# Splitting the last list of expert slots: broken slots first, full ones after the copy to the output

## The chip, the cores and the metric

The kernel runs on one core of a Trainium2 chip. Times are device microseconds of one execution. A core has five engines with a queue each: TensorE (PE in the profile, its weight loads PEld), VectorE (DVE), ScalarE (ACT), GpSimd (POOL) and SyncE (SP). SP issues most plain DMAs, POOL issues the indirect ones: a gather of rows by a list of indices, and a store that adds to the rows it names.

## What is computed

One decoder layer on 16 sequences of 128 tokens of 256 numbers, in float32: attention over latents, a recurrent mixing with a context, and a mixture of 8 experts, each behind a layer norm, each added to its input. Only the last matters here. Every token goes to its two best experts:

```python
logits = x @ router_w.T
routing_weights, selected = sparsemixer_eval(logits, JITTER_EPS)   # two of 8 experts a token
for e in range(E):
    h = jax.nn.silu(x @ w_gate[e].T) * (x @ w_up[e].T)
    out = out + dense_w[:, e:e + 1] * (h @ w_down[e].T)
return x + out
```

That gives 4096 entries (token, expert) for the 2048 tokens. How many an expert gets is known only at run time.

## The kernel before

**Steps.** The program is one loop over steps s, written out in full. Steps 0 to 63 are the attention's units (four a sequence); mixing, layer norm and routing of a sequence follow some steps behind its attention. From step 64 (SLOT0) on, each step also does one *slot* of the experts: up to 128 entries of one expert. In each step there are four places, "pre", "A", "B" and "C", in which a plan (`at(step, place, function)`) hangs further work. Every engine works off its instructions in the order of this loop; no scheduler moves them.

**Lists.** Routing (`route`) writes each entry (token, weight) to its expert's list in DRAM, with indirect DMAs of POOL. The sum before the experts lies in the DRAM tensor `acc`, its normed rows in `xn2`. Which expert and which part of its list a slot takes is worked out at run time on VectorE by `table`, in some twenty small instructions that are spread over several places. `list_slots` then reads the start of a slot's entries into registers and loads the 128 entries (SP, L849).

**Tables.** Because at least so many full slots are sure once 8 and 12 sequences are routed, the first 17 slots (SF) are taken early, from tables "0" and "1". When all are routed there are two more tables. Table "3" has 8 slots (S3) that are certainly full. Table "2" has 14 (S2): all that is left, each expert's remaining full slots and then its broken one, and as many of the 14 as there are entries for. Table "3" runs last. Of table "2", 11 slots always run (an unused one works on blank entries) and the last 3 (`RARE`, SKIP = 3) stand under a run-time condition, `if_used`, which compares the number of used slots with k on all five engines. A skipped slot's body is replaced by instructions that raise the semaphores as the body would have. So 17 + 11 + 8 = 36 slots always run, in the order of `ORDER`, and the three guarded ones are placed between the 28th and the 29th of them.

**One slot.** In step j of the slots: `fetch` gathers the rows of the slot three places ahead (POOL, L898, into xr); `bring` copies the next slot's expert weights (ACT and DVE, L920); `up` makes the products pg and pu (PE, L966), SiLU (ACT, L976) and hT (DVE, L978); then come the works of place "C"; `turn` transposes the next slot's rows (PE, L928) and copies them to xT (DVE, L930); `down` makes the last product pd of the slot before (PE, L988), scales it to y (DVE, L999) and adds it to its rows (POOL, L1004). Place "B" stands ahead of fetch, bring and up. `turn` of the slot after and `down` of the slot before thus lie between two `up`s on TensorE.

**The copy.** The adding stores of all slots but the last 8 go to `acc`. At the first of the last 8, SP copies `acc` to the output (L1001, 2 MB from DRAM to DRAM), and these 8 add to the output itself. Every add waits for the one before it, since both may name the same row. `y` has three buffers, `xr` four.

The diff touches the tables (`last_table`, `very_last`), the guard (`if_used`), `down` and the plan.

Of the kernel before, what the change touches and what calls it, by code (L numbers as in the profile page):

```python
# [9 lines left out]
F32 = mybir.dt.float32  # L10
# [8 lines left out]
P = 128  # L19
B = 16  # L20
T = 128
N = B * T
C = 256
# [3 lines left out]
E = 8  # L27
# [25 lines left out]

def sure(b):
    return (2 * b * T - E * (P - 1) + P - 1) // P

# [1 line left out]
FIRST_B = (8, 12)  # L60
S1 = [sure(FIRST_B[0]), sure(FIRST_B[1]) - sure(FIRST_B[0])]
SF = sum(S1)
S3 = 8
assert SF + S3 <= sure(B)
S2 = (2 * N + E * (P - 1)) // P - SF - S3
NS = SF + S2 + S3


SKIP = 3
RARE = range(SF + S2 - SKIP, SF + S2)  # L70
ORDER = [j for j in range(NS) if j not in RARE]

SLOT0 = NU
# [6 lines left out]
def decoder_kernel(  # L80
# [19 lines left out]
    nc = tc.nc  # L100

    const = ctx.enter_context(tc.tile_pool(name="const", bufs=1))
# [25 lines left out]
    def bank(tag, name, bufs=2):  # L128
        return psum.tile([P, 512], F32, tag=tag, name=name, bufs=bufs)
# [68 lines left out]
    ebase = const.tile([P, E], F32, tag="ebase", name="ebase")  # L198
    before = const.tile([P, P], F32, tag="before", name="before")
    ones = const.tile([P, P], F32, tag="ones", name="ones")  # L200
    iotas = const.tile([P, max(*S1, S2, S3)], F32, tag="iotas", name="iotas")
    seg = const.tile([P, E], F32, tag="seg", name="seg")

    taken = const.tile([P, E], F32, tag="taken", name="taken")
# [30 lines left out]
    def constants():  # L235
        for t, step, base in ((rev, -1, E), (eid, 1, 0), (ebase, N, 0)):
            nc.gpsimd.iota(
                t,
                pattern=[[step, E]],
                base=base,  # L240
                channel_multiplier=0,
                allow_small_or_imprecise_dtypes=True,
            )

        nc.gpsimd.memset(before, 1.0)
        nc.gpsimd.affine_select(
            out=before,
            in_=before,
            compare_op=ALU.is_gt,
            fill=0.0,  # L250
            base=0,
            pattern=[[1, P]],
            channel_multiplier=-1,
        )
        nc.gpsimd.memset(ones, 1.0)
        nc.gpsimd.iota(
            iotas,
            pattern=[[1, max(*S1, S2, S3)]],
            base=0,
            channel_multiplier=0,  # L260
            allow_small_or_imprecise_dtypes=True,
        )
        nc.gpsimd.memset(seg, 1.0)
        nc.gpsimd.memset(taken, 0.0)

        nc.gpsimd.memset(blank, 0)
        place = blank[:, :, 1]
        nc.gpsimd.iota(place, pattern=[[1, QL]], base=0, channel_multiplier=QL)
        nc.vector.tensor_single_scalar(place, place, P - 1, ALU.bitwise_and)
        nc.vector.tensor_single_scalar(place, place, N, ALU.bitwise_or)  # L270
# [478 lines left out]
    def whole(c, add, name):  # L749

        f = rp.tile([P, E], F32, tag=f"wf{name}", name=f"wf{name}")
        nc.vector.tensor_scalar_add(f, c, float(add))
        i = rp.tile([P, E], I32, tag=f"wi{name}", name=f"wi{name}")
        nc.vector.tensor_copy(i, f)
        nc.vector.tensor_single_scalar(i, i, 7, ALU.logical_shift_right)
        nc.vector.tensor_copy(f, i)
        return f
# [111 lines left out]
    def last_table():  # L869

        cnt = counts("2")
        full = whole(cnt, 0, "3")
        nc.vector.tensor_sub(full, full, took[0])
        yield
        last = share(full, S3, "3")
        both = rp.tile([P, E], F32, tag="both", name="both")
        nc.vector.tensor_add(both, took[0], last)
        took.append(last)
        yield
        left = whole(cnt, P - 1, "2")  # L880
        nc.vector.tensor_sub(left, left, both)
        yield from table(S2, left, both, "2")

    making = {}

# [21 lines left out]
    hpools, xTs, hTs, regs, useds, brought = [], {}, {}, {}, [], {}  # L907
# [22 lines left out]
        nc.vector.tensor_copy(xT, pt[:, : NC * P].rearrange("p (c t) -> p c t", c=NC))  # L930
        xTs[j] = xT

    def if_used(j, work):

        t, k = slots[j]
        if not useds:
            _, v = nc.values_load_multi_w_load_instructions(
                t["used"],
                engines=[
                    mybir.EngineType.PE,  # L940
                    mybir.EngineType.Activation,
                    mybir.EngineType.DVE,
                    mybir.EngineType.Pool,
                    mybir.EngineType.SP,
                ],
                min_val=0,
                max_val=S2,
                skip_runtime_bounds_check_because="no more than all",
            )
            useds.append(v[0])  # L950
        with tc.If(useds[0] > k):
            work(j)

    def up(j):
        t, k = slots[j]
# [25 lines left out]
    def down(j):  # L981
        e = regs.pop(j)
        hT = hTs.pop(j)
        pd = bank("mm", f"pd_{j}")

        def products():
            for f in range(NF):
                nc.tensor.matmul(  # L988
                    pd[:, :C],
                    hT[:, f, :],  # L990
                    wall[:, bass.ds(e, 1), WD0 + f * C : WD0 + (f + 1) * C],
                    start=(f == 0),
                    stop=(f == NF - 1),
                )

        products()
        en = entries.pop(j)
        y = hpools[0].tile([P, C], F32, tag="y", name=f"y_{j}", bufs=3)
        nc.vector.tensor_scalar_mul(y, pd[:, :C], en[:, 2:3].bitcast(F32))  # L999
        if j == SF + S2:  # L1000
            nc.sync.dma_start(out2, acc[0:N, :])  # L1001

        def add():
            nc.gpsimd.indirect_dma_start(  # L1004
                out=acc if j < SF + S2 else out2,
                out_offset=bass.IndirectOffsetOnAxis(ap=en[:, 1:2], axis=0),
                in_=y,
                in_offset=None,
                compute_op=ALU.add,
            )  # L1010

        add()


    plan = {}
# [1 line left out]
    def at(step, place, fn, *args):  # L1017
        plan.setdefault((step, place), []).append((fn, args))
# [106 lines left out]
    for b in range(B):  # L1125
        s = NHG * b
        if b + 1 < B:
            at(s + 2, "pre", load_ctx, b + 1)
        at(s + 1, "C", wkv_exps, b)
        at(s + 2, "B", wkv_back, b)  # L1130
        at(s + 3, "A", wkv_back_add, b)
        at(s + 4, "B", wkv_forth, b)
        at(s + 5, "A", wkv_forth_add, b)
        at(s + 5, "B", project, b, (0, 1))
        at(s + 6, "B", project, b, (2, 3))
        at(s + 6, "C", rest_values, b)
        at(s + 7, "B", project, b, (4, 5))
        at(s + 7, "C" if b < B - 1 else "B", project, b, (6, 7, NP))
        for name, (step, place) in {B - 2: last_but_one, B - 1: last}.get(b, usual).items():
            at(s + step, place, stages[name], b)  # L1140
        if b < E:
            for k in range(3):
                at(s + 11 + k, "C", load_expert, b, k)
        if b % RB == RB - 1:
            r = b // RB
            parts = ((13, "B"), (13, "C"), (14, "B"), (15, "B"), (15, "C"))
            if b == B - 1:
                parts = ((12, "B"), (12, "C"), (13, "B"), (14, "B"), (14, "C"))
            for step, place in parts:
                at(s + step, place, route_part, r)  # L1150
            for k in range(2 * RB):
                if b < B - 1:
                    at(s + 16 + k, "A", route_part, r)
                else:
                    at(s + 15 + k // 4, "AC"[k // 2 % 2], route_part, r)
        if b + 1 in FIRST_B:
            i = FIRST_B.index(b + 1)
            for k in range(6):
                at(s + 18 + k, "C", table_part, i, first_table, i)
            for k in range(0, S1[i], 2):  # L1160
                at(s + 24 + k // 2, "C", list_slots, min(2, S1[i] - k))
        if b == B - 1:
            for k in range(7):
                at(s + 15 + k // 3, "ABC"[k % 3], table_part, "2", last_table)
            for k in range(0, S2, 4):
                at(s + 17 + k // 4, "C", list_slots, min(4, S2 - k))
            for k in range(4):
                at(s + 20 + k, "B", table_part, "3", very_last)
            for k in range(0, S3, 4):
                at(s + 24 + k // 4, "C", list_slots, min(4, S3 - k))  # L1170
    for j in range(AHEAD):
        at(SLOT0 - 2 + (j + 1) // 2, "A", fetch, j)

# [31 lines left out]
    def whole_slot(j):  # L1205
        fetch(j)
        bring(j)
        turn(j)
        up(j)
        down(j)  # L1210

    for s in range(SLOT0 + len(ORDER) + 1):
        j = s - SLOT0
# [44 lines left out]
        if j >= 0:  # L1258
            ahead(j + 1, turn)
            if j >= 1:  # L1260
                down(ORDER[j - 1])
        if j == SF + S2 - SKIP:
            for r in RARE:
                if_used(r, whole_slot)
    assert not plan and len(slots) == NS


# [52 lines left out]
```

## Time and profile before

| | us |
|---|---|
| median of three runs | 571.44 |
| lowest, highest | 567.83, 572.62 |
| the profiled execution's own time | 571.29 |
| its span in the profile | 569.6 |

```profile
PE 523.7 (92%) x3317; PEld 447.1 (78%) x3334; DVE 326.8 (57%) x831; ACT 293.7 (52%) x891; POOL 326.6 (57%) x379
## 2 busy tenths in 40 slices
PE   4989999999999999999998959989999999998990
...
POOL 5355656574787665688636873544486545451532
PEclk9999999999999999999997979999999999999996
```

The first line is the busy time of each engine, its share of the span and its instructions. The digits below are busy tenths of 40 equal slices of 14.2 us. TensorE's dip in the middle (slices 23 to 26) is where attention ends and the slots begin. The last slices are the slots alone.

The group of the products shows how many slots ran: 576 matmuls of one kind, 16 for each slot, so 36, and none of the guarded three.

```profile
L966 PE MATMUL pg<-xT,w 128*128 128x128 f32 x576 | 72.5, 280 | 11.7 <-DVE xT L930 9.8
L1004 POOL DMA_INDIRECT acc<-y,en x28 | 47.7, 1705 | 60.9 <-DVE y L999 27.5
```

### The profile page before, as it was taken

How to read it: one execution, taken by the hardware profiler on the slowest of the kernel's cores; microseconds unless marked ns; L12 is line 12 of the kernel's file. 1: busy time of each engine (PE TensorE's matmuls, PEld its weight loads, DVE VectorE, ACT ScalarE, POOL GpSimd, SP SyncE). 2: the span in 40 equal slices, each digit the busy share in tenths (PEclk: the TensorE clock that was granted, in tenths of full speed). 3: DMA queues.
4: the chain of work that ended last, by engine and by line, in shares of the span. 5: the costliest groups of instructions: out<-in, count | busy, mean ns of one | idle time of the engine just before them, and what ended most of it. 6: DMA issues, size and time to landing. Idle time of an engine off the chain costs nothing. (4 is left out here: it accounts for less than half of the span.)

```text
span 569.6 us, 10246 instructions
## 1 busy us (share of the span) xinstructions
PE 523.7 (92%) x3317; PEld 447.1 (78%) x3334; DVE 326.8 (57%) x831; ACT 293.7 (52%) x891; POOL 326.6 (57%) x379
## 2 busy tenths in 40 slices
PE   4989999999999999999998959989999999998990
PEld 3767788877877877878876648879989999998990
DVE  3435576577886678878668745555563543433330
ACT  1667776786676777767774744332322323222300
POOL 5355656574787665688636873544486545451532
PEclk9999999999999999999997979999999999999996
DMA  4422145364455544121221111233223333235321
GB/s 144 116 66 74 56 139 181 100 184 126 131 146 152 153 137 150 58 76 40 66 66 44 36 48 30 53 56 57 39 30 50 58 57 47 48 51 171 51 36 18
DMA packets 39662, 47.59 MB, mean 84 GB/s; under 512 B 14136, under 2 KB 31416, under 8 KB 39576
## 3 DMA queue, kind: packets, MB, share of 16 engines
q1 hardware_dynamic: 30106, 37.20, 22.3%
q0 software_dynamic: 7936, 9.51, 10.7%
q8 instruction: 28, 0.46, 0.4%
q10 hardware_dynamic: 1566, 0.21, 0.2%
q14 instruction: 26, 0.21, 0.1%
HBM read 28.22 MB, written 13.31 MB: 73 GB/s over the span
## 5 line engine op out<-in xcount | busy, mean ns | idle before, releaser
L466 POOL TENSOR_TENSOR pr<-pr,rsum 128x512 f32<-128x512 f32 x64 | 76.6, 1197 | 37.2 <-DVE rsum L465 27.8
L453 ACT ACTIVATE pr<-ps,nm 128x128 f32<-128x128 f32 x256 | 90.9, 372 | 10.2 <-DVE nm L445 10.1
L976 ACT ACTIVATE sl<-pg 128x512 f32<-128x512 f32 x36 | 21.5, 598 | 132.4 <-PE pg L966 128.4
L966 PE MATMUL pg<-xT,w 128*128 128x128 f32 x576 | 72.5, 280 | 11.7 <-DVE xT L930 9.8
L966 PEld LDWEIGHTS pg<-xT,w 128*128 128x128 f32 x576 | 70.7, 196 | 15.4 <-issue 14.1
L1004 POOL DMA_INDIRECT acc<-y,en x28 | 47.7, 1705 | 60.9 <-DVE y L999 27.5
L433 PEld LDWEIGHTS ps<-kvT,q 72*128 72x128 f32 x512 | 67.5, 191 | 16.2 <-issue 8.0
L506 PE MATMUL po<-outw_sb,yP 128*128 128x256 f32 x288 | 74.6, 387 | 0.0
L978 DVE TENSOR_TENSOR hT<-sl,pu 128x512 f32<-128x512 f32 x36 | 24.8, 688 | 86.1 <-PE pu L966 80.0
L433 PE MATMUL ps<-kvT,q 72*128 72x128 f32 x512 | 68.8, 276 | 4.3 <-DMA q<-qr 3.1
L966 PE MATMUL pu<-xT,w 128*128 128x128 f32 x576 | 70.5, 276 | 0.0
L988 PE MATMUL pd<-wall,hT 128*128 x288 | 68.0, 379 | 0.0
L966 PEld LDWEIGHTS pu<-xT,w 128*128 128x128 f32 x576 | 67.6, 193 | 0.0
L480 PE MATMUL py<-aT,kvN 128*72 128x512 f32 x128 | 66.6, 602 | 0.3 <-ACT aT L474 0.3
L445 DVE TENSOR_REDUCE nm<-ps 128x4 f32<-128x512 f32 x64 | 43.7, 683 | 37.7 <-PE ps L433 37.7
L398 PE MATMUL pq<-xnT,wq_sb 128*128 128x256 f32 x256 | 64.9, 385 | 0.0
L506 PEld LDWEIGHTS po<-outw_sb,yP 128*128 128x128 f32 x288 | 54.6, 194 | 12.2 <-issue 5.3
L474 ACT COPY aT<-pt 128x512 f32<-128x512 f32 x64 | 37.3, 583 | 44.4 <-PE pt L472 44.1
L988 PEld LDWEIGHTS pd<-wall,hT 128*128 128x128 f32 x288 | 52.0, 190 | 5.6
L453 ACT ACTIVATION_READ_ACCUMULATOR pr<-ps,nm 128x1 f32 x256 | 53.8, 210 | 0.0
L398 PEld LDWEIGHTS pq<-xnT,wq_sb 128*128 128x128 f32 x256 | 45.9, 194 | 4.9 <-issue 0.2
L898 POOL DMA_INDIRECT xr<-xn,en x36 | 37.2, 1034 | 13.4 <-issue 7.4
(171 smaller groups left out, 861.3 us busy)
## 6 DMA issues: line engine op xcount, KB each, us to landing
wall<-in_wg_dram SPq DMA_DIRECT2D x8, 512.0 KB
wall<-in_wu_dram SPq DMA_DIRECT2D x8, 512.0 KB
wall<-in_wd_dram SPq DMA_DIRECT2D x8, 512.0 KB
q<-q SPq DMA_DIRECT2D x16, 224.0 KB
yP<-yB SPq DMA_DIRECT2D x32, 112.0 KB
cx<-in_cx_dram SPq DMA_DIRECT2D x16, 128.0 KB
acc<-x SPq DMA_DIRECT2D x16, 128.0 KB
xn<-row SPq DMA_DIRECT2D x16, 128.0 KB
```

The source lines that it names most:

```text
L398: nc.tensor.matmul(pq[:, :GT], w[:, c, :], xnT[g][:, c, :], start=(c == 0), stop=(c == NC - 1))
L433: nc.tensor.matmul(ps[:, j, :], q[g, hg][0:L, j, ts(i, T)], kvT[g][:, ts(i, T)], start=False, stop=(j == HG - 1),)
L445: nc.vector.tensor_reduce(nm, ps, AX.X, ALU.max, negate=True)
L453: nc.scalar.activation(pr[:, j, :], ps[:, j, :], AF.Exp, bias=nm[:, j : j + 1], accum_out=sums[:, j : j + 1],)
L466: nc.gpsimd.tensor_mul(pr, pr, rsum.unsqueeze(2).to_broadcast([P, HG, T]))
L474: nc.scalar.copy(aT, pt)
L480: nc.tensor.matmul(py[:L], kvN[g][:, ts(i, L)], aTs.pop((b, hg)), start=True, stop=True)
L506: nc.tensor.matmul(pos[b][:, :C], yP[b][:, i, :], outw_sb[:, i, :], start=(i == 0), stop=(i == NP))
L898: nc.gpsimd.indirect_dma_start(out=xr, out_offset=None, in_=xn2[0 : t["rows"], :], in_offset=bass.IndirectOffsetOnAxis(ap=entries[j][:, 0: ...
L966: nc.tensor.matmul(o[:, ts(f, P)], w[:, c * F + f * P : c * F + (f + 1) * P], xT[:, c, :], start=(c == 0), stop=(c == NC - 1),)
L988: nc.tensor.matmul(pd[:, :C], hT[:, f, :], wall[:, bass.ds(e, 1), WD0 + f * C : WD0 + (f + 1) * C], start=(f == 0), stop=(f == NF - 1),)
L1004: nc.gpsimd.indirect_dma_start(out=acc if j < SF + S2 else out2, out_offset=bass.IndirectOffsetOnAxis(ap=en[:, 1:2], axis=0), in_=y, in_of ...
```

## The change

Table "2" is split in two. The new table "2" has 8 slots, one for each expert's rest (broken or empty). A new table "4" has 7 (S4 = 32 - 25): the full slots that table "3" leaves. Order and target of the adds become: 17 early slots and 8 rests to `acc`, then the copy, then up to 7 open full slots and the 8 last ones to the output. Of the open ones (`OPEN`) the first three always run, but their adding store stands under the run-time condition; the last four (`RARE`) stand under it whole. There are 40 slots (NS) instead of 39, and again 36 that always run.

The condition (now `used`, which returns the comparison) is first loaded at the first open slot's add. Counted from step 64, table "4" is made in place "C" of slot steps 14 to 18 (19 is empty), table "3" moves from place "B" of slot steps 16 to 19 to place "C" of 20 to 23, and the loads of its entries go from slot steps 20 and 21 to 24 and 25.

```diff
-S3 = 8
-S2 = (2 * N + E * (P - 1)) // P - SF - S3
-NS = SF + S2 + S3
-SKIP = 3
-RARE = range(SF + S2 - SKIP, SF + S2)
+S2 = E
+S3 = sure(B) - SF
+S4 = 2 * N // P - SF - S3
+NS = SF + S2 + S4 + S3
+SKIP = S4 - 3
+OPEN = range(SF + S2, SF + S2 + S4)
+RARE = OPEN[S4 - SKIP :]
...
         cnt = counts("2")
         full = whole(cnt, 0, "3")
+        yield
+        left = whole(cnt, P - 1, "2")
+        nc.vector.tensor_sub(left, left, full)
+        fulls.append(full)
+        yield from table(S2, left, full, "2")
+
+    def open_table():
+
+        full = fulls.pop()
         nc.vector.tensor_sub(full, full, took[0])
-        yield
         last = share(full, S3, "3")
         both = rp.tile([P, E], F32, tag="both", name="both")
         nc.vector.tensor_add(both, took[0], last)
         took.append(last)
         yield
-        left = whole(cnt, P - 1, "2")
-        nc.vector.tensor_sub(left, left, both)
-        yield from table(S2, left, both, "2")
+        nc.vector.tensor_sub(full, full, last)
+        yield from table(S4, full, both, "4")
...
-        add()
+        if j in OPEN and j not in RARE:
+
+            with tc.If(used(j)):
+                add()
+        else:
+            add()
...
-            for k in range(4):
-                at(s + 20 + k, "B", table_part, "3", very_last)
-            for k in range(0, S3, 4):
-                at(s + 24 + k // 4, "C", list_slots, min(4, S3 - k))
+            for k in range(6):
+                at(s + 18 + k, "C", table_part, "4", open_table)
+            for k in range(4):
+                at(s + 24 + k, "C", table_part, "3", very_last)
+            for n, step in ((S4, s + 24), (S3, s + 28)):
+                for k in range(0, n, 4):
+                    at(step + k // 4, "C", list_slots, min(4, n - k))
...
-        if j == SF + S2 - SKIP:
+        if j == RARE[0]:
             for r in RARE:
-                if_used(r, whole_slot)
+                with tc.If(used(r)):
+                    whole_slot(r)
```

More of the change, by code (lines that the diff above doesn't have):

```diff
@@ L62 @@
 SF = sum(S1)
-S3 = 8
-assert SF + S3 <= sure(B)
-S2 = (2 * N + E * (P - 1)) // P - SF - S3
-NS = SF + S2 + S3
-SKIP = 3
-RARE = range(SF + S2 - SKIP, SF + S2)
+S2 = E
[5 more added lines that the diff above has]
+RARE = OPEN[S4 - SKIP :]
 ORDER = [j for j in range(NS) if j not in RARE]
@@ L200, in decoder_kernel @@
     ones = const.tile([P, P], F32, tag="ones", name="ones")
-    iotas = const.tile([P, max(*S1, S2, S3)], F32, tag="iotas", name="iotas")
+    iotas = const.tile([P, max(*S1, S2, S3, S4)], F32, tag="iotas", name="iotas")
     seg = const.tile([P, E], F32, tag="seg", name="seg")
@@ L257, in constants @@
             iotas,
-            pattern=[[1, max(*S1, S2, S3)]],
+            pattern=[[1, max(*S1, S2, S3, S4)]],
             base=0,
@@ L879, in last_table @@
         yield
-        left = whole(cnt, P - 1, "2")
-        nc.vector.tensor_sub(left, left, both)
-        yield from table(S2, left, both, "2")
+        nc.vector.tensor_sub(full, full, last)
+        yield from table(S4, full, both, "4")
+    fulls = []
     making = {}
@@ L931, in turn, with used @@
         xTs[j] = xT
-    def if_used(j, work):
+    def used(j):
         t, k = slots[j]
@@ L946, in if_used @@
                 min_val=0,
-                max_val=S2,
+                max_val=S4,
                 skip_runtime_bounds_check_because="no more than all",
@@ L950, in if_used @@
             useds.append(v[0])
-        with tc.If(useds[0] > k):
-            work(j)
+        return useds[0] > k
     def up(j):
```

## The prediction

> **What bounds the kernel now.** I read the slice table first: from slice 30 on TensorE is at 9 tenths or more with the clock granted in full, so the phase after about 430 us is bound by TensorE. Below, "place n" is the n-th of the 36 slots that always run (0 to 35, in the order of ORDER), and "row(n)", "y(n)", "add(n)" are its gather of rows, its scaled result and its adding store. The chain of waits (start, length, what) ends so:
>
> ```profile
> 550.09 1.79 PE pu L966 x16
> 551.88 3.47 PE pd L988 x16
> 555.35 0.02 issue
> 555.37 0.50 DVE y L999
> 555.87 0.27 issue
> 556.14 3.72 DMA out_dram<-y,en
> ```
>
> It follows TensorE back, place by place, in steps of 5.52 us, to an idle time at 514.96. But it passes over the second limit. The timeline of POOL, with the copy from the timeline of SP:
>
> ```profile
> 497.29 1.78 POOL L1004 DMA_INDIRECT acc<-y,en  x1 [2.43 <-DVE y L999]
> ...
> 513.85 1.59 POOL L1004 DMA_INDIRECT acc<-y,en  x1 [2.20 <-DVEq L951]
> 519.77 1.00 POOL L898 DMA_INDIRECT xr<-xn,en  x1 [4.33 <-PE pxr L928]
> 528.35 1.58 POOL L1004 DMA_INDIRECT out_dram<-y,en  x1 [7.58 <-DVE w L920]
> 530.23 1.00 POOL L898 DMA_INDIRECT xr<-xn,en  x1 [0.30 <-PE pxr L928]
> 532.83 1.59 POOL L1004 DMA_INDIRECT out_dram<-y,en  x1 [1.59 <-DVE y L999]
> ...
> 556.14 1.55 POOL L1004 DMA_INDIRECT out_dram<-y,en  x1 [2.98 <-DVE y L999]
> 560.61 1.56 POOL L1004 DMA_INDIRECT out_dram<-y,en  x1 [2.92 <-DMA out_dram<-y,en]
> ```
> ```profile
> 518.80 0.62 SPq L1001 DMA_DIRECT2D out_dram<-acc  x1
> ```
>
> The first row is add(24), 513.85 is add(27), 519.77 row(32), 528.35 add(28), and the last two are add(34) and add(35). The copy starts 4.95 us after add(27), once that has landed, and add(28) stands until the copy has landed, 14.50 us after add(27) started. From there each add waits for the one before to land: seven steps from 528.35 to 560.61, 4.61 us each, faster than TensorE's 5.52 but not fast enough to use up the delay in eight slots. y(34) was there at 553.65 + 0.48 = 554.13; add(34) left at 556.14. So POOL's queue of adds ends the kernel, 1.7 us behind what TensorE would allow, and anything that moves add(28) moves the end.
>
> The line of the guarded slots (L951) and the idle times of TensorE from its timeline:
>
> ```profile
> L951 PEldq COMPARE_BRANCH  x3: 219/368/457, 510.5 to 514.0; - x3
> L951 POOLq COMPARE_BRANCH  x3: 45/45/53, 514.2 to 517.1; - x3
> L951 POOLq INC_SWDGE_SEM  x3: 1160/1174/1217, 514.5 to 517.7; - x3
> ```
> ```profile
> 418.93 2.02 PE L966 MATMUL pg<-xT,w 128*128 128x128 f32 x16 [1.11 <-DVE xT L930]
> ...
> 514.96 2.02 PE L966 MATMUL pg<-xT,w 128*128 128x128 f32 x16 [1.92 <-DVEq L951]
> ```
>
> A skipped slot costs POOL one INC_SWDGE_SEM of 1.17 us (starts 1.6 us apart) and TensorE a share of 1.92 us.
>
> **The change, part by part.** The work stays 36 slots. I worked out the routing from the reference's inputs: the experts get 544, 511, 479, 525, 488, 402, 612 and 535 entries, which makes 28 full slots and 8 broken ones. Before: 17 + 11 + 8, the three guarded ones skipped. After: 17 early, 8 rests, 28 - 25 = 3 open ones (their guarded adds all run, all four guarded slots are skipped), 8 last. TensorE's products are the same.
>
> *Table work on VectorE.* The stall at 418.93 comes from nine small instructions between hT at 415.98 and xT at 418.37. They put xT off by 1.79 us and TensorE stood 1.11, so xT has 0.68 us to spare. The new table "2" leaves two instructions there (0.24 us apart for 64 elements, by the rows at 447): the 1.11 goes, nothing is late next. But tables "4" and "3" now stand between hT and xT in ten parts; table "3" stood ahead of hT before, where VectorE idles 2.5 us, and cost nothing. The parts priced by the same instructions in VectorE's timeline: six to split the full slots 1.00 us (413.24 to 414.24), five with the first compare 0.88 (417.49 to 418.37), two groups of five with products 1.04 each (452.79 to 453.83); the others 0.4 to 0.6, within the 0.68. Over the spare time: 0.32 + 0.20 + 0.36 + 0.36 = 1.24. Net **+0.13 us** on all that follows.
>
> *SP.* Eight entry loads move from slot steps 20 and 21 to 24 and 25, and one is added, for the 40th slot. After its table the last eight took 458.84 to 464.16, 0.66 us each; now they run from about 485 to 490.5. row(28) leaves at 493.9, and the copy that stands behind them on SP not before 502: hidden, with 3 us over. Behind the copy SP has only a register load and branches.
>
> *The copy, three places earlier.* It waits for add(24) in place of add(27). add(24) goes at 497.29 + 0.13 = 497.42; with the same 14.50 us add(25) starts at 511.92, then add(26) 516.5 and add(27) 521.1 by the 4.61 step. Behind these on POOL are the gathers: row(30) leaves at 511.92 + 1.89 = 513.8, lands 3.7 us later (the landing of the gathers from 490 to 512) at 517.5, needed at 519.4; row(31) lands at 522.1, needed at 524.9. row(32) beside the copy took 8.0 us to land before; now row(29), at 499.5, is the nearest to it and is not needed until 511. Three buffers of y: y(28), due at about 521.5, needs add(25) landed (516.5); later ones have more.
>
> *The guards around add(25) to add(27)* put a register load and seven branches on every engine where three skips stood. No taken guard is in the trace. TensorE's sequencer had reached the first branch at 510.5, with products still to run until 513.04: it is 2.5 us ahead and a compare takes at most 0.46, so I take 0; the upper end is 0.46 for each of two, and a gain is excluded, since they only add. On POOL 0.05 each, within the 3 us wait for the add before to land.
>
> *Four skipped slots for three.* TensorE resumes when VectorE is through; VectorE's skips are 0.65 us apart (its semaphore waits of L951 run from 513.7 to 515.0: two steps): 1.92 becomes 2.57, +0.65. On POOL, add(27) to row(32) was 5.92 us with three; with four 5.92 + 1.6 = 7.52. So row(32) leaves at 521.1 + 7.52 = 528.65 and add(28) 1.3 us behind it (1.00 and a gap of 0.30) at **529.95, where it was 528.35: +1.6 us**. All seven adds behind it follow.
>
> TensorE meanwhile: row(32) lands at 532.35; its transpose, at 529.64 before, is due at 529.64 + 0.13 + 0.65 = 530.4, a new stall of 1.9. Its last product ends 2.7 us later, y(34) at 556.8, add(34) not before 557.1; POOL's queue reaches it at 529.95 + 6 x 4.61 = 557.6. POOL still ends it. So the earlier copy wins nearly nothing: three more adds stand behind it, 13.8 us at 4.61 against 16.55 us of TensorE time, and the fourth skip takes the rest back.
>
> [...] The trace has the compare at 45 ns on POOL, but 1.17 us in the instruction that makes up the skipped semaphore counts. [...]
>
> The profiled run took 571.29 for a span of 569.6 and lies 0.15 under the median of 571.44: 571.44 + 1.6 = **573.0 us**.
>
> **Rivals.** [...]
>
> [...]
>
> (3) *The change doesn't do what the counts say.* Expert 1 has 511 entries, one short of a fourth full slot. In the reference token 1286 misses it by 0.0003 in the logit. With 512 there are 29 full slots and the fourth open one runs unpipelined: its gather stands behind add(27) on POOL, leaves at 523.0 and lands at 526.7; transpose and xT 0.6, products 3.6, hT 0.7, product 1.7 and y 0.5 take it to 533.8, where TensorE would have gone on at 515.7: 18 us, about 588. Before would not have changed (511 and 512 both make four slots).
>
> (4) *Costs of the main case add up*: the copy a microsecond slower, the guards 1, the skips 2 us each on POOL (2 more): 575 to 577.
>
> **How the numbers follow.** Main case 0.53 (571.5 to 575); rival 1 0.21; rival 4 0.13; rival 2 0.07; rival 3 0.03; 0.03 for a gain that I don't see: TensorE's own gaps and tail hold at most 4 us. The range 569.5 to 577.0 holds the main case, rival 1 with the half per cent by which the runs differ (567.83 to 572.62), and rival 4. Over 1% (5.7 us, about what a measurement of this kernel can tell from no change): slower 0.14 (rivals 2 and 3 and the end of 4), faster 0.03, within 0.83.
>
> **What would show it.** Right: no idle at the 418.93 matmul and four idles of 0.2 to 0.4 us between 433 and 485; the copy issued near 502; eleven adds to the output, the first near 512; four INC_SWDGE_SEM; a stall of TensorE on row(32) of about 2 us; add(28) near 530. Wrong: add(28) before 527; TensorE idle behind add(25) or add(26); a product in a guarded slot (over 576 matmuls into pg).

## The result, and the profile after

| | before | after |
|---|---|---|
| median | 570.37 us (22 runs) | 573.31 us (22 runs) |
| lowest, highest | 567.00, 572.62 | 570.35, 575.77 |
| profiled execution, its span | 571.29, 569.6 | 572.08, 570.3 |

The ratio is 1.0051 (95% interval 1.0034 to 1.0067): slower by half a per cent, 2.9 us, against a forecast of +1.6 us and 573.0. A later comparison (after_again below) gave 1.0039 (1.0018 to 1.0061).

The two profiled executions differ by 0.8 us only, since each execution begins its slots at a slightly different time (hT of place 11 starts at 415.98 in before, at 415.34 in after). So I measure from VectorE's hT of place 11 (both kernels reach it 6.28 us behind the hT of place 10), and cut the rest into stages by rows of VectorE's and GpSimd's timelines. hT(24) to add(24) is 8.15 to 8.16 us in every run below and is left out of the columns, but is in the last one.

| us | hT(11) to hT(24) | add(24) to add(28) | add(28) to add(35) | hT(11) to add(35) |
|---|---|---|---|---|
| before | 73.15 | 31.06 | 32.26 | 144.63 |
| after | 74.03 | 31.62 | 32.26 | 146.06 |
| forecast for after | 73.28 | 32.53 | 32.26 | 146.2 |

The stages add 0.88 and 0.56: +1.43 us, close to the +1.6 forecast, but put together differently. What each stage looks like:

*Places 12 to 24.* TensorE's timeline of after, at the place where before stood still for 1.11 us (418.93), and the three idle times that the new table work leaves:

```profile
417.02 1.95 PE L976 MATMUL pg<-xT,w 128*128 128x128 f32 x16
...
434.02 2.02 PE L976 MATMUL pg<-xT,w 128*128 128x128 f32 x16 [0.28 <-DVE xT L941]
451.49 2.02 PE L976 MATMUL pg<-xT,w 128*128 128x128 f32 x16 [0.30 <-DVE xT L941]
479.88 2.02 PE L976 MATMUL pg<-xT,w 128*128 128x128 f32 x16 [0.32 <-DVE xT L941]
```

The bracket is the idle time ahead of the group and what ended it. The long stall is gone, as forecast, and three of the four short ones are there. They sum to 0.90, but the stage lost more than that: against before, hT gains 1.4 us at places 12 and 13 and gives back 2.3 by place 24, in steps of 0.2 to 0.6 at five of the nine places with parts of tables 4 and 3. The idle times alone would have hidden more than half of it.

*The copy and the skips.* GpSimd's timeline of after, then SyncE's, then the line of the guarded slots:

```profile
497.52 1.78 POOL L1015 DMA_INDIRECT acc<-y,en  x1 [2.43 <-DVE y L1009]
...
510.79 1.59 POOL L1015 DMA_INDIRECT out_dram<-y,en  x1 [10.18 <-DMA out_dram<-acc]
...
516.35 1.66 POOL L1015 DMA_INDIRECT out_dram<-y,en  x1 [2.67 <-DVEq L1283]
...
520.89 1.59 POOL L1015 DMA_INDIRECT out_dram<-y,en  x1 [1.58 <-issue]
527.84 1.00 POOL L909 DMA_INDIRECT xr<-xn,en  x1 [5.35 <-PE pxr L939]
529.14 1.58 POOL L1015 DMA_INDIRECT out_dram<-y,en  x1 [0.30 <-issue]
```
```profile
501.55 0.62 SPq L1012 DMA_DIRECT2D out_dram<-acc  x1
```
```profile
L1283 POOLq INC_SWDGE_SEM  x4: 1160/1183/1217, 521.1 to 525.7; - x4
```

497.52 is add(24). The copy leaves at 501.55, add(25) starts at 510.79, add(27) at 520.89. Between add(27) and row(32) (527.84) GpSimd does no data work: it goes through four guarded slots, with one compare of 45 to 50 ns and one INC_SWDGE_SEM of 1.2 us in each (durations are minimum, median and maximum in ns, then first and last start). In before, three of them stood at the same place, but ahead of the wait for the copy. Now nothing is left to wait for behind them: add(28) goes 0.3 us after the gather. SyncE's entry loads were through at 489.75 (23 from 430.50 on), long before the copy was due.

*TensorE at the skips.* Its timeline and its stretches (after a stretch and its length come the busy times of PE, PEld, DVE, ACT and POOL, then the granted clock, the DMA share and GB/s):

```profile
515.75 2.46 PE L976 MATMUL pg<-xT,w 128*128 128x128 f32 x16 [2.47 <-PEq L1283]
518.01 3.18 PE L976 MATMUL pu<-xT,w 128*128 128x128 f32 x16
```
```profile
510.00:513.00 3.00, 3.00 (x22) 2.72 (x21) 1.02 (x2) 0.18 (x1) 1.91 (x2) 1.00 0.09 8
...
516.00:518.00 2.00, 2.00 (x16) 2.00 (x16) 0.53 (x1) 0.53 (x1) 1.66 (x1) 0.79 0.00 0
518.00:520.00 2.00, 2.00 (x12) 2.00 (x11) 0.00 (x0) 1.53 (x2) 1.00 (x2) 0.50 0.57 66
520.00:522.00 2.00, 2.00 (x14) 1.92 (x14) 0.71 (x2) 0.00 (x0) 1.11 (x1) 0.86 0.24 66
```

The idle time of 2.47 us was forecast (2.57). The next two groups of products were not: they took 2.46 and 3.18 us where such a group takes 1.95 to 2.02, at a granted clock of down to 0.50 (1.00 again from 522 on). It puts TensorE 1.6 us further back, so that it ties with GpSimd at the end:

```profile
556.06 0.48 DVE L1009 TENSOR_SCALAR y<-pd,en 128x256 f32<-128x256 f32 x1 [0.97 <-PE pd L998]
```
```profile
556.82 1.56 POOL L1015 DMA_INDIRECT out_dram<-y,en  x1 [3.06 <-DVE y L1009]
561.40 1.56 POOL L1015 DMA_INDIRECT out_dram<-y,en  x1 [3.02 <-DMA out_dram<-y,en]
```

y(34) is there at 556.54, add(34) leaves at 556.82 and add(35), which waits for its landing, 4.58 us later at 561.40.

*The guards.* TensorE's line of the guards around add(25) to add(27), and the group of the products:

```profile
L1025 PEldq COMPARE_BRANCH  x6: 65/134/307, 499.7 to 510.4; - x6
```
```profile
L976 PE MATMUL pg<-xT,w 128*128 128x128 f32 x576 | 73.3, 282 | 12.2 <-DVE xT L941 9.6
```

The compares lie under products that run (TensorE has no idle time between 499 and 513), and 576 products are 36 slots: no 29th full one.

### The profile page after: what moved, and what is told of

It is laid out like the page before. It is cut to its first block, busy times and chain, and to the rows that moved or that the text cites. A ratio compares the mean times of both kernels' runs of the same rounds, so it can differ in the third digit from the quotient of the medians.

```text
span 570.3 us, 10306 instructions
## 1 busy us (share of the span) xinstructions
PE 527.5 (92%) x3317; PEld 449.1 (79%) x3334; DVE 328.2 (58%) x848; ACT 294.0 (52%) x891; POOL 326.9 (57%) x379
## 5 line engine op out<-in xcount | busy, mean ns | idle before, releaser
L1015 POOL DMA_INDIRECT acc<-y,en x25 | 42.3, 1693 | 53.7 <-DVE y L1009 23.2
L976 PE MATMUL pu<-xT,w 128*128 128x128 f32 x576 | 71.8, 279 | 0.0
L976 PEld LDWEIGHTS pu<-xT,w 128*128 128x128 f32 x576 | 69.0, 196 | 0.0
```

The source lines that it names most:

```text
L976: nc.tensor.matmul(o[:, ts(f, P)], w[:, c * F + f * P : c * F + (f + 1) * P], xT[:, c, :], start=(c == 0), stop=(c == NC - 1),)
L1015: nc.gpsimd.indirect_dma_start(out=acc if j < SF + S2 else out2, out_offset=bass.IndirectOffsetOnAxis(ap=en[:, 1:2], axis=0), in_=y, in_of ...
```

## The experiments

My theory after the profile: (a) the table parts at place "C" cost TensorE 2.3 us and the removed stall gives 1.4 back; (b) the skips, which lay beside the copy, now lie on GpSimd's path; (c) the guards around the adds cost nothing. Rivals: the guards stop an engine; TensorE (with its half clock) and not GpSimd's queue sets the end; nothing but four skips for three matters. All ratios are to the kernel before on the same chip in the same comparison.

### First comparison: tables, and the number of skips

a_tables_b, the parts of tables 4 and 3 at place "B" of the slot step, so that they stand ahead of VectorE's wait for hT's operands:

```diff
-                at(s + 18 + k, "C", table_part, "4", open_table)
+                at(s + 18 + k, "B", table_part, "4", open_table)
...
-                at(s + 24 + k, "C", table_part, "3", very_last)
+                at(s + 24 + k, "B", table_part, "3", very_last)
```

> The changed kernel with the parts of tables 4 and 3 moved from between hT and xT to the place ahead of hT. Theory A (small vector work ahead of xT stalls TensorE): the three idle times of 0.3 us go, and hT of place 24 stands 2.3 us earlier against hT of place 14 than in the changed kernel; copy, adds and the end follow, about 2 us less than the changed kernel (571.3 where that is 573.3). Rival B (TensorE is not the limit there, the end is set by the skips alone): the stalls go but the end moves less than 0.7 us.

a_three_skips: six open slots, three of them guarded whole slots (as many skips as before). a_no_skips: three open slots, no guarded one:

```diff
-S4 = 2 * N // P - SF - S3
+S4 = 6
```
```diff
-S4 = 2 * N // P - SF - S3
+S4 = 3
...
-        if j == RARE[0]:
+        if RARE and j == RARE[0]:
```

> The changed kernel with six open slots instead of seven, so that three guarded slots are skipped instead of four. Theory A (the fourth skip takes the idle of TensorE from 1.9 to 2.5 us, which the clock gate answers with half clock, and POOL 1.6 us more): idle near 1.9 us, clock at 1.00, TensorE's end 2.2 us earlier, POOL's row(32) 1.6 us earlier, end 1.5 to 2.2 us lower. Rival C (the clock dip is chance and comes with three skips as well): TensorE gains 0.6 us only, end about 1 us lower.

> The changed kernel with three open slots instead of seven: the four guarded slots that no expert uses on these inputs are not in the program. Theory A (skips cost TensorE an idle of 2.5 us and 1.7 us of half clock behind it, POOL 6.9 us): TensorE's last product ends about 4.2 us earlier, the granted clock stays at 1.00 behind place 28, add(28) comes 2.4 us earlier; the end is then set by TensorE and lies 3 to 4 us lower. Rival B (the guards around the adds cost most): less than 1 us.

b_four_skips: the kernel before with a fourth guarded slot.

```diff
-S2 = (2 * N + E * (P - 1)) // P - SF - S3
+S2 = (2 * N + E * (P - 1)) // P - SF - S3 + 1
...
-SKIP = 3
+SKIP = 4
```

> The kernel before with a 15-slot table 2 and four guarded slots instead of three, none of them used. Theory A: the idle of TensorE goes from 1.9 to 2.5 us and the clock halves behind it, TensorE ends 2.2 us later; row(32) leaves 1.6 us later, beside the copy; add(28) still waits for the copy, so the end moves by 1 to 2.5 us. Rival C (no clock dip): 0.6 us on TensorE and less than 0.5 us on the end.

This comparison ran on another chip, where the kernel before took 576.2 us, and all four profiles have a long disturbance at 421 to 435 us that before and after do not have (its rows are in the last section). hT(11) to hT(14) took 23.2 to 25.4 us there, against 17.97 in before and 16.56 in after. The ratios, 1.0040 (1.0022 to 1.0058) for a_tables_b, 1.0037 (1.0020 to 1.0054) for a_three_skips, 1.0019 (0.9997 to 1.0041) for a_no_skips and 1.0023 (1.0000 to 1.0046) for b_four_skips, mix that with the edits. I read the stages behind it instead:

| us | hT(14) to hT(24) | add(24) to add(28) | TensorE idle at the skips | hT(14) to add(35) |
|---|---|---|---|---|
| before (as above) | 55.18 | 31.06 | 1.92 | 126.66 |
| after (as above) | 57.47 | 31.62 | 2.47 | 129.50 |
| a_tables_b | 55.18 | 31.90 | 2.41 | 127.28 |
| a_three_skips | 57.47 | 30.07 | 1.83 | 128.30 |
| a_no_skips | 57.37 | 27.94 | none | 126.45 |
| b_four_skips | 55.19 | 32.69 | 2.44 | 127.53 |

The first column settles (a): with the parts at "B" the stage is as long as before, at "C" it is 2.2 to 2.3 us longer, whatever else is edited. The rows are those of hT(14) and hT(24) in VectorE's timeline of a_tables_b:

```profile
441.39 0.69 DVE L988 TENSOR_TENSOR hT<-sl,pu 128x512 f32<-128x512 f32 x1 [4.58 <-PE pu L976]
...
496.57 0.69 DVE L988 TENSOR_TENSOR hT<-sl,pu 128x512 f32<-128x512 f32 x1 [2.39 <-PE pu L976]
```

The second column settles (b): with the copy placed early, none, three and four skips give 27.94, 30.07 and 31.6 to 31.9. The last column says how much of it reached the end: 2.2 us from the move of the tables alone, 1.2 from three skips for four, 3.1 from none. In the case without skips the queue of adds still sets the end (y(34) is there at 561.96, add(34) leaves at 563.73). A fourth skip in the kernel before costs add(28) as much, 1.63 us (0.9 at the last add), so there too the skips were on the path. That I had not seen. SyncE's timeline of b_four_skips and its line of the guarded slots show why:

```profile
522.86 0.62 SPq L1001 DMA_DIRECT2D out_dram<-acc  x1
```
```profile
L951 POOLq INC_SWDGE_SEM  x4: 1160/1178/1213, 517.0 to 521.7; - x4
```

The last INC_SWDGE_SEM starts at 521.7 and ends 1.18 later, at 522.9: the copy leaves at that moment. In before the third one starts at 517.7 and ends at 518.9, and the copy leaves at 518.80. The copy waited for GpSimd's skips, and not only for add(27). The half clock behind the skips was in none of these profiles (groups at 2.0 us, idle 2.41 to 2.44).

### Second comparison: the skips moved under the wait, and the guards

On another chip than the first comparison (before: 569.87 us median). after_again is the changed kernel itself.

> The changed kernel itself, beside the variants of this call, so that each can be set against it on one chip. If the change costs the same on any chip: ratio to the kernel before 1.004 to 1.007, as in the first comparison (1.0051). If part of that 0.5% came from where this chip or this build places things in memory: within 0.2% of 1.000. The profile, if TensorE's half clock behind the skipped slots follows from the four skips: matmuls into pg and pu near 516 to 518 again at 2.4 and 3.2 us; if it is chance, at 2.0. If the long stalls at slot steps 12 and 13 (421 to 435 us, seen in the four profiles of the first call) belong to the chip and not to the variants, they show again here.

a_skips_early: the four guarded slots stand ahead of add(25), right behind the issue of the copy, in place of behind add(27).

```diff
...
-        if j == SF + S2:
-            nc.sync.dma_start(out2, acc[0:N, :])
...
-        if j == RARE[0]:
+        if j == SF + S2:
+            nc.sync.dma_start(out2, acc[0:N, :])
             for r in RARE:
                 with tc.If(used(r)):
                     whole_slot(r)
```

> The copy to the output and the four guarded slots stand ahead of add(25), so that GpSimd works through the four skips (about 6.7 us) while it would wait for add(24) and the copy anyway (13 us). Theory 1, GpSimd's queue alone sets the end: add(28) follows add(27) after 4.6 us in place of 8.2, and the kernel ends 3.6 us earlier (-0.6% against the changed kernel of this call). Theory 2, TensorE and GpSimd's queue tie (y(34) ended 556.55, add(34) started 556.82 in the profile after): add(28) comes 3.6 us earlier but add(34) and add(35) don't move by more than 0.5 us, since y(34) is not earlier; a gain only where TensorE's slow matmuls behind the skips (1.6 us) go. Theory 3, the copy comes late: with the skips ahead of it, if add(25) starts later than 13.5 us behind add(24), GpSimd's skips are not covered and there is a loss.

a_best: a_skips_early and the edit of a_tables_b together.

> a_skips_early with the parts of tables 4 and 3 moved to the place in the slot step (between up and down) where VectorE idles. If the late xT of those ten parts cost TensorE 2.3 us, as the profile after reads, and TensorE sets the end once GpSimd's skips are covered: 2 to 3 us under a_skips_early and under the kernel before (ratio 0.995 to 0.998). If the parts cost nothing that reaches the end: the same as a_skips_early. If the table's later end makes the lists late (en of slot 28 lands after its gather is due): slower than a_skips_early by over 1 us, with GpSimd waiting on a load of en near 494.

a_plain_adds: no guards around the adds.

```diff
-        if j in OPEN and j not in RARE:
+        if False:
```

> The changed kernel without the guards around add(25), add(26) and add(27): the adds always run; for these inputs all three are taken, so the output is the same. My step 4 said that a taken guard costs nothing: within 0.1% of the changed kernel in this call. [...]

| | median us | ratio (95%) | hT(11) to hT(24) | add(24) to add(28) | add(28) to add(35) | hT(11) to add(35) |
|---|---|---|---|---|---|---|
| after_again | 572.33 | 1.0039 (1.0018 to 1.0061) | 74.02 | 31.95 | 31.78 | 145.91 |
| a_plain_adds | 572.76 | 1.0048 (1.0025 to 1.0071) | 74.03 | 32.19 | 31.63 | 146.01 |
| a_skips_early | 572.15 | 1.0025 (1.0003 to 1.0047) | 74.22 | 29.06 | 34.71 | 146.15 |
| a_best | 569.25 | 0.9973 (0.9948 to 0.9999) | 71.74 | 29.64 | 34.08 | 143.62 |

(c) holds: without the guards around the adds the kernel is 0.4 us slower, inside the interval, and its stages are the same.

a_skips_early is the theory of the tie, theory 2 of its expectation: against after_again, add(28) comes 2.9 us sooner after add(24), and the last add comes 0.2 us later. GpSimd's timeline of a_skips_early, add(28) and then the last two:

```profile
526.96 1.58 POOL L1012 DMA_INDIRECT out_dram<-y,en  x1 [1.48 <-issue]
...
557.17 1.56 POOL L1012 DMA_INDIRECT out_dram<-y,en  x1 [3.74 <-DVE y L1009]
561.67 1.56 POOL L1012 DMA_INDIRECT out_dram<-y,en  x1 [2.94 <-DMA out_dram<-y,en]
```

The adds now wait for y: TensorE sets the end in place of GpSimd. In this profile TensorE also lost 1.7 us to the half clock, which after_again did not have; the medians, 0.2 us apart (the ratios 0.8, with intervals that overlap), say that the edit alone is worth little. In an execution without the half clock it may be worth more: best_again below, without it, is 1.3 us shorter in the stages than a_best, the same kernel with it. The table work counts in full: a_best is 2.9 us under a_skips_early (2.5 by the stages) and a little under the kernel before. It counts without the early skips too, as the 2.2 us of a_tables_b show, since add(24), and with it the copy, follows hT(24) (by 8.15 to 8.16 us in every run).

### Third comparison: what bounds the better version

On a further chip (before: 570.37 us median). b_no_skips is the kernel before without guarded slots, best_none is a_best without them; best_again is a_best; best_fill adds two small products behind each skip.

```diff
-S2 = (2 * N + E * (P - 1)) // P - SF - S3
+S2 = 11
...
-SKIP = 3
+SKIP = 0
...
-        if j == SF + S2 - SKIP:
+        if RARE and j == SF + S2 - SKIP:
```

> The kernel before without its three guarded slots (11 slots in the middle table, none guarded; for these inputs the output is the same). Theory 1, in the kernel before the skips lie under the wait for the copy: row(32) leaves GpSimd at 519.8 and add(28) waits until 528.4 for the copy whatever the skips do, so TensorE gains its 1.9 us of idle but the seven adds behind the copy start where they did: 0 to 0.4 us faster (ratio 0.999 to 1.000). Theory 2, TensorE sets the end there too: 1.9 us faster (0.9967).

```diff
-S4 = 2 * N // P - SF - S3
+S4 = 3
```

> a_best without its four guarded slots (three open ones, none guarded; for these inputs the output is the same). If TensorE sets the end of a_best, its 2.45 us of idle at the skips and, in those executions that have them, up to 1.6 us of half clock behind them go straight off the end: 2.4 to 4.0 us under a_best of this call. The eleven adds then stand in GpSimd's queue at 4.55 us from about 509.0 to 554.5, so the gain can't be over 4.9. If GpSimd's queue sets the end of a_best: under 0.5 us.

```diff
                 with tc.If(used(r)):
                     whole_slot(r)
+                fill = bank("mm", f"fill_{r}")
+                for _ in range(2):
+                    nc.tensor.matmul(fill[:, :P], ident, ident, start=True, stop=True)
```

> a_best with two small matmuls of the identity behind each skipped slot, which nothing reads; they break TensorE's idle of 2.45 us into pieces. If the half clock behind the skips (pg at 3.2 and 3.6 us in place of 2.0 in two profiles of the last call) follows from TensorE standing idle in one stretch: pg and pu behind the skips at 2.0 us, and 0.5 to 1.5 us under a_best of this call, less what the small matmuls cost (each skip waits for the matmuls ahead of it to end: 0.2 to 0.5 each). If the half clock comes from something else: the profile may still show it, and the kernel is 1 to 2 us slower than a_best.

> a_best once more: ratio to the kernel before 0.995 to 0.9999 again if its gain is real and holds on this chip too; and the profile shows whether the half clock behind the skips is there each time (2 of 2 profiles with the skips moved early had it, 1 of 5 with the skips behind add(27)).

| | median us | ratio (95%) | hT(11) to hT(24) | add(24) to add(28) | add(28) to add(35) | hT(11) to add(35) |
|---|---|---|---|---|---|---|
| b_no_skips | 568.90 | 0.9982 (0.9961 to 1.0003) | 73.11 | 29.54 | 31.92 | 142.73 |
| best_again | 568.88 | 0.9974 (0.9951 to 0.9997) | 71.73 | 29.05 | 33.34 | 142.28 |
| best_none | 567.59 | 0.9940 (0.9920 to 0.9960) | 71.74 | 28.08 | 33.03 | 141.01 |
| best_fill | 569.29 | 0.9980 (0.9955 to 1.0005) | 71.74 | 29.24 | 35.02 | 144.16 |

b_no_skips missed its expectation: 1.5 us faster by the medians and 1.9 by the stages, not 0 to 0.4; the ratio's interval just holds 1. It is not TensorE, though, that gave it (theory 2). GpSimd's and SyncE's timelines:

```profile
510.83 1.79 POOL L1004 DMA_INDIRECT acc<-y,en  x1 [2.18 <-DVE y L999]
...
523.82 1.58 POOL L1004 DMA_INDIRECT out_dram<-y,en  x1 [9.89 <-DMA out_dram<-acc]
```
```profile
514.82 0.62 SPq L1001 DMA_DIRECT2D out_dram<-acc  x1
```

The copy leaves 3.99 us after add(27), where it took 4.95 with three skips and 6.44 with four (516.42 to 522.86). That is the wait for the skips once more, and it was worth 1.0 us in the kernel before; the other 0.5 lies between the copy's issue and add(28) (9.0 us against 9.55).

best_none gains 1.3 us over best_again, less than the 2.4 to 4.0 that TensorE's idle alone would give. Its y(34) in VectorE's timeline, and its last adds in GpSimd's, say where it stops:

```profile
551.16 0.48 DVE L1009 TENSOR_SCALAR y<-pd,en 128x256 f32<-128x256 f32 x1 [0.97 <-PE pd L998]
```
```profile
553.51 1.55 POOL L1012 DMA_INDIRECT out_dram<-y,en  x1 [2.87 <-DVE y L1009]
558.07 1.56 POOL L1012 DMA_INDIRECT out_dram<-y,en  x1 [3.00 <-DMA out_dram<-y,en]
```

y(34) is there at 551.64 and add(34) leaves at 553.51, 4.42 behind add(33): the queue of adds is the bound again. best_fill has no half clock, but neither had best_again, so it says nothing on what brings the half clock on; the small products stretch the time between a slot's last product and the next slot's first from 2.7 us (493.26 to 495.98 in best_again) to 4.5 (493.28 to 497.74), and bring no gain.

a_best was measured twice, at 0.9973 and 0.9974, with both intervals just below 1: by the ratios 1.5 us faster than the kernel before (by the medians 0.6 and 1.5), and by the medians 3.1 us faster than the changed kernel.

## Why the prediction was right, and where it was not

The sign and the time (573.0 against 573.31) were right, the time in part by luck: the change was 2.9 us, not 1.6, and the three runs that the forecast starts from have a median 1.07 us above that of all 22. By the steps of the forecast:

- *Table work, net +0.13.* The mechanism was right; the term that was mis-sized is xT's spare time. I took 1.79 us late less 1.11 idle, 0.68. But in before the step from hT(11) to hT(12) took 6.87 where others take 5.52, 1.35 more, which the idle time does not show in full. VectorE's timeline of before with hT(11), the xT behind it and hT(12), then that of after with hT(14), its xT and hT(15):

```profile
415.98 0.69 DVE L978 TENSOR_TENSOR hT<-sl,pu 128x512 f32<-128x512 f32 x1 [1.04 <-PE pu L966]
...
418.37 0.42 DVE L930 COPY xT<-pxr 128x256 f32<-128x256 f32 x1
...
422.85 0.69 DVE L978 TENSOR_TENSOR hT<-sl,pu 128x512 f32<-128x512 f32 x1 [0.70 <-PE pu L966]
```

```profile
431.90 0.69 DVE L988 TENSOR_TENSOR hT<-sl,pu 128x512 f32<-128x512 f32 x1 [2.37 <-PE pu L976]
...
433.45 0.41 DVE L941 COPY xT<-pxr 128x256 f32<-128x256 f32 x1
...
437.93 0.69 DVE L988 TENSOR_TENSOR hT<-sl,pu 128x512 f32<-128x512 f32 x1 [3.07 <-PE pu L976]
```

  With nothing between them, xT stands 0.60 behind hT, so at place 14 of after it is 0.95 late, and the next hT 0.51 (6.03 against 5.52): 0.44 was to spare. Each later place with a delay gives 0.44 or 0.45, and so does before (1.79 less 1.35). The lengths of the parts were right within 0.06. The four groups that I had over the spare time cost 1.99 in place of 1.24, the five smaller parts 0.28 in place of nothing, and the removed stall gave 1.42 (73.15 to 71.73) in place of 1.11: the stage lost 0.88.
- *The copy, "with the same 14.50 us".* This step failed. add(24) to add(25) took 13.27 in after and 13.40 in after_again. I read the 4.95 us from add(27) to the copy in before as add(27)'s landing. 1.0 of it was the wait for the third skip (3.99 in b_no_skips), and the moved copy stands ahead of the skips. The gain didn't last: add(26) came 5.56 after add(25) in place of 4.61, and add(27) was where the sum had it, 520.89 against 521.1. Every profile with the early copy has that longer step (5.5 to 6.2 us), the two without skips too; why it is longer is open.
- *The guards at 0.* Right, by the trace (TensorE has no idle time between 499 and 513) and by a_plain_adds (0.4 us slower without them, inside the interval). The stop of an engine at a taken guard, rival 2 of the chances (0.07), is shown by no run.
- *Four skips for three, 1.6.* Right in place and price: 1.63 in the kernel before, 1.55 to 2.1 with the early copy (a_three_skips against after and its twins). The sum had add(27) to row(32) at 7.52; it was 6.95. So add(28) came at 529.14, not 529.95.
- *INC_SWDGE_SEM, 1.17 us a skip.* The row of before held: the four of after took 1.16 to 1.22 (the compare itself 45 to 50 ns on GpSimd). The gain of rival 1 in the chances (0.21), by skips that hide in add(27)'s landing, is shown by no run: with four skips in that place add(28) came 8.25 us behind add(27) in after, and without skips 4.78 (a_no_skips).
- *A new stall of 1.9 on row(32).* Absent in after, where TensorE was later by the half clock; 0.50 in after_again, 0.90 in a_plain_adds. Over-sized, and off the path.
- *The half clock* was in no step of the forecast. It brought TensorE to a tie with GpSimd in that profile.

So the total agreed partly because two sizes erred in opposite directions: tables 0.75 too low, copy and skips 0.9 too high. The stages account for 1.3 to 1.4 us. The medians say 2.5 and 2.9 (intervals 1.0 to 3.5 and 1.9 to 3.8). What makes up the rest is open. The half clock is a weak candidate: after has it, and its last column is only 0.15 us above that of after_again, which has none. A better one lies ahead of hT(11). From the start of ScalarE's 40th-last row of pr, in the attention, to that of its last one takes 45.1 to 45.3 us in eight profiles (before, after and after_again among them), 43.5 to 43.6 in four of the changed kernel's variants, and 41.8 to 42.1 in b_no_skips and b_four_skips, though no edit rewrites that stretch. How often each kernel takes which, fourteen profiles can't say.

## What to carry to other kernels

Before you move a DMA or a wait, list what its semaphore waits for: here each skipped block cost the queue that issues its DMAs an INC_SWDGE_SEM of 1.2 to 1.9 us, and in the kernel before the copy, which waits for an add on that queue, waited for the skips as well (it left 3.99 us behind add(27) without skips, 4.95 with three, 6.44 with four). Put such a block under a wait that must be served anyway. Put small work of a helper engine where that engine idles, not ahead of the operand that the busiest engine needs next (2.3 us here), and take what a delay costs from the step between two like rows, not from the idle time alone. When two engines tie at the end, an edit that relieves only one of them can show next to nothing (0.2 us by the medians in a_skips_early).

## What the hardware showed that I had not expected

**Half clock behind 2.5 us of idle time, in some executions.** Eight profiles have TensorE idle for 2.41 to 2.72 us at four skips; in three of them (after, a_skips_early, a_best) a stretch at half clock follows. TensorE's timeline and stretches of a_best, and the same place in best_again:

```profile
497.31 3.64 PE L976 MATMUL pg<-xT,w 128*128 128x128 f32 x16 [2.45 <-DVEq L1281]
```
```profile
497.30:499.00 1.70, 1.69 (x8) 1.70 (x9) 0.69 (x1) 0.79 (x1) 0.00 (x0) 0.50 0.69 81
499.00:501.00 2.00, 2.00 (x12) 2.00 (x12) 0.00 (x0) 0.02 (x1) 0.00 (x0) 0.58 0.41 132
```
```profile
495.98 2.02 PE L976 MATMUL pg<-xT,w 128*128 128x128 f32 x16 [2.72 <-PEq L1281]
```

The clock column gives the length, if the clock was either 1.00 or 0.50, the lowest value there: in a_best (1.70 x 0.50 + 2.00 x 0.42) x 2 = 3.4 us at half clock, in after (0.21 + 0.50 + 0.14) x 2.00 x 2 = 3.4, and in a_skips_early (1.50 x 0.29 + 2.00 x 0.50 + 2.00 x 0.14) x 2 = 3.4, so 1.7 us lost each time. The idle times ahead of it were 2.44 to 2.47 us. That the gap brings it on is not shown: five profiles with gaps of 2.41 to 2.72 had no half clock, nor had the two with three skips (1.83 and 1.92).

**Skips are dearer at the earlier place.** INC_SWDGE_SEM took 1.16 to 1.22 us behind add(27) (before, after, b_four_skips), but 1.87 to 1.91 when the four stood ahead of add(25) (a_best, best_again). The line of the skips in best_again, and the copy in SyncE's timeline:

```profile
L1281 POOLq INC_SWDGE_SEM  x4: 1871/1878/1907, 494.7 to 501.4; - x4
```
```profile
497.98 0.62 SPq L1279 DMA_DIRECT2D out_dram<-acc  x1
```

The copy is not the cause: the first of the four took at least 1.87 us from 494.7 and was over before the copy left. The cause is open. The skips were still covered: in a_best row(29) left at 505.82, and add(25) had to wait for the copy until 509.00.

**A disturbance on one chip.** On the chip of the first comparison, engines that wait for TensorE went on late at slot steps 12 and 13. TensorE's and ScalarE's timelines of a_no_skips:

```profile
427.51 1.95 PE L976 MATMUL pu<-xT,w 128*128 128x128 f32 x16
...
435.13 2.26 PE L976 MATMUL pg<-xT,w 128*128 128x128 f32 x9 [3.62 <-DVE xT L941]
```
```profile
433.00 0.60 ACT L986 ACTIVATE sl<-pg 128x512 f32<-128x512 f32 x1 [11.46 <-PE pd L998]
```

The products that sl needs (pg, at 425.65 for 2.02 us) were through by 427.7, and sl ran at 433.00, hT at 433.96. It was so, with other lengths, in all four profiles on that chip (5.2 to 8.8 us more from hT(11) to hT(14) than in the kernel of the same table layout on the other chips) and in none of the others. It belongs to no edit; its cause is open.
